# An attention GRU: its SBUF pools reordered, keys transposed two steps ahead, groups gathered a step ahead

## The chip, the cores and the metric

One core of a Trainium2 chip. The metric is the device time of one execution in microseconds (us), median of several runs. The experiments ran in three sessions, each on a chip of the same kind (called the second, third and fourth chip here; the record does not say whether one of them is the chip of the first measurement). Each session ran the kernel before beside the experiments, so only ratios within one chip are compared. All profiled runs quoted here were in the fast state (granted TensorE clock 0.994 to 0.996 over the whole execution).

## The reference, cut to what matters

For 1024 users with up to T = 100 past items each, a GRU runs over the items; its states are the *keys*. An attention gives each step a weight, and a second GRU, the AUGRU, runs over the keys:

```python
def augru_step(h, inp):
    x_t, a_t = inp                       # key and attention weight of step t
    ti = jnp.concatenate([h, x_t], axis=-1)
    r = jax.nn.sigmoid(ti @ aug_Wr.T + aug_br)
    u = jax.nn.sigmoid(ti @ aug_Wu.T + aug_bu)
    h_hat = jnp.tanh(jnp.concatenate([h * r, x_t], axis=-1) @ aug_Wh.T + aug_bh)
    u = a_t[:, None] * u
    h_new = (1.0 - u) * h + u * h_hat
    return (h_new, h_new)
```

The state after a user's last step goes, with other features, through three small layers to a score. Everything is in float32.

## The kernel before

The users are sorted by length and split into two halves of 512 (`NH = 2`), which take turns: a *half-step* is one step of one half. Ended users drop out on the right, so that a step works on `widths[t]` columns, from 512 down to 96. In the profiles a matmul in float32 stands as two records on the matmul engine (PE), each with a weight load (the page counts 8320 of each). Twelve of them make a half-step: `ph` is closed with `r` of the other half, then `pr` and `pu` with `h`, then three gates of the next half-step are opened with its key `k`.

```python
    def augru_phase(pools, widths, alive):
        wp = pools.enter_context(tc.tile_pool(name="wp3", bufs=3))
        qp = pools.enter_context(tc.tile_pool(name="qp3", bufs=3 * NH))
        sp = pools.enter_context(tc.tile_pool(name="sp3", bufs=2))
        kp = pools.enter_context(tc.tile_pool(name="kp3", bufs=4))

        ps = [
            pools.enter_context(tc.tile_pool(name=f"ps3_{n}", bufs=1, space=PSUM))
            for n in range(7)
        ]
        pa = pools.enter_context(tc.tile_pool(name="pa3", bufs=1, space=PSUM))
        # ... cut ...
        def load_key(t, i, n=None):          # cut: the first four lines
            k = qp.tile([P, HB], F32, name="k3")
            if q < WHOLE:                # steps 0 to 7: PE transposes, ACT copies
                p = pa.tile([P, HB], F32, tag="a", name="pk3") if n is None else bank("pk3", n)
                for g in range(-(-w // P)):
                    nc.tensor.transpose(p[:, ts(g, P)], r[:, g, ts(m, P)], ident)
                nc.scalar.copy(k[:, :w], p[:, :w])
            else:                        # from step 8 on: DVE transposes
                w = -(-w // R)
                nc.vector.transpose(
                    k.rearrange("p (k r) -> p k r", r=R)[:, :w, :], r[:, :w, ts(m, R)]
                )
            keys[t, i] = k
        # ... cut ...
        def half_step(t, i):
            w, h = widths[t], h3[i][:, : widths[t]]
            before, after = ((t - 1, 1), (t, 1)) if i == 0 else ((t, 0), (t + 1, 0))
            if before in resets:
                open_state(*before)
            pr = close_gate(t, i, "pr", wr, h)
            pu = close_gate(t, i, "pu", wu, h)
            nc.scalar.activation(pr, pr, AF.Sigmoid, bias=later["br"])
            nc.scalar.activation(pu, pu, AF.Sigmoid, bias=later["bu"])
            state = states.pop(1 - i, None)
            if state is not None:
                nc.vector.tensor_mul(state[0], state[0], state[1])
            r = wp.tile([P, HB], F32, name="r3")[:, :w]
            nc.vector.tensor_mul(r, h, pr)
            if state is not None:
                nc.vector.tensor_sub(state[3], state[0], state[2])
            if t == 1 and i == 0:
                store_weights(0, pa.tile([P, HB], F32, tag="a", name="pw"))
                first_state(1, spare)
            elif t == 1:
                first_weights(1, spare)
            nc.vector.tensor_mul(pu, pu, att.pop((t, i))[:, :w])
            rest = wp.tile([P, HB], F32, name="rest")[:, :w]
            nc.vector.scalar_tensor_tensor(
                out=rest, in0=pu, scalar=1.0, in1=h, op0=ALU.subtract, op1=ALU.mult
            )
            later["pace"] = rest[:, 0:1]
            resets[t, i] = r, pu, rest
            if after[0] < T and (*after, "pr") not in opened:
                open_gates(*after)
            if t == 1 and i:
                store_weights(1, spare)
            if t + 2 < T:
                load_att(t + 2, i)
            if 1 < t < T - 1:
                load_key(t + 1, i)
```

The tiles that the keys are transposed from (`rows`) come by indirect transfers that POOL issues (`gathers`), 32 for a group of eight steps, spread over the half-steps before. The GRU that runs before the AUGRU has its own pools; a tile of a new pool that lies over an old pool's space waits until that space is free (in the profile before, ACT's first key copy stands idle 8.44 us for POOL's `pooled`). Its six PSUM banks belong to one pool:

```python
        ps = pools.enter_context(tc.tile_pool(name="ps", bufs=6, space=PSUM))
```

Of the kernel before, what the change touches and what calls it, by code (L numbers as in the profile page):

```python
# [9 lines left out]
F32 = mybir.dt.float32  # L10
# [9 lines left out]
P = 128  # L20
B = 1024
T = 100
HB = 512
NH = B // HB
# [31 lines left out]
FIRST = [sum(READ[:q]) for q in range(len(READ))]  # L56
# [18 lines left out]
def kernel(ctx: ExitStack, tc: tile.TileContext, a: dict, out: bass.AP):  # L75
# [96 lines left out]
    def all_of(steps):  # L172
        for _ in steps:
            pass
# [762 lines left out]
    def augru_phase(pools, widths, alive):  # L937


        wp = pools.enter_context(tc.tile_pool(name="wp3", bufs=3))  # L940
        qp = pools.enter_context(tc.tile_pool(name="qp3", bufs=3 * NH))
        sp = pools.enter_context(tc.tile_pool(name="sp3", bufs=2))
        kp = pools.enter_context(tc.tile_pool(name="kp3", bufs=4))

# [11 lines left out]
        def bank(name, n=None):  # L956

            if n is None:
                n = ring.pop(0)
                ring.append(n)  # L960
            return ps[n].tile([P, HB], F32, tag="g", name=name)

        def first_step(i):

            k = keys.pop((0, i))
            gates = []
            for j, (n, f) in enumerate((("u", AF.Sigmoid), ("h", AF.Tanh))):
                p = bank(f"p{n}", EARLY_BANKS[NH * i + j])
                nc.tensor.matmul(p, lhsT=later["w" + n][:, 1, :], rhs=k, start=True, stop=True)
                gate = sp.tile([P, HB], F32, name=f"first_{n}")  # L970
                nc.scalar.activation(gate, p, f, bias=later["b" + n])
                gates.append(gate)
            return gates
# [18 lines left out]
        def first_state(i, p):  # L992
            weight_row(0, i, p)
            u, h = gates[i]
            nc.vector.tensor_mul(p, p, u)
            nc.vector.tensor_mul(h3[i], p, h)

        def first_weights(i, p):
            weight_row(1, i, p)
            at = att[1, i] = wp.tile([P, HB], F32, name="at", bufs=6)  # L1000
            nc.scalar.copy(at, p)

        def store_weights(i, p):

            for g in range(GH):
                nc.tensor.transpose(p[:, ts(g, P)], sorted_rows[i][:, g, :], ident)
            rows_t = wp.tile([P, HB], F32, name="att_t", bufs=2)
            nc.vector.tensor_copy(rows_t, p)
            nc.sync.dma_start(out=att_d[i], in_=rows_t[:T, :])
            load_att(2, i)  # L1010

        def load_att(t, i):
            w = widths[t]
            at = wp.tile([P, HB], F32, name="at", bufs=6)
            nc.sync.dma_start(
                out=at[:, :w], in_=att_d[i][t, :w].partition_broadcast(P)
            )
            att[t, i] = at

        def load_key(t, i, n=None):  # L1020

            q = max(j for j, first in enumerate(FIRST) if first <= t)
            w, m, r = widths[t], t - FIRST[q], rows[q, i]
            k = qp.tile([P, HB], F32, name="k3")
            if q < WHOLE:
# [4 lines that stand above are left out]
            else:  # L1030
# [6 lines that stand above are left out]
        def open_gates(t, i, banks=(None,) * 3):  # L1037

            k = keys.pop((t, i))[:, : widths[t]]
            for m, name, n in zip((wr, wh, wu), ("pr", "ph", "pu"), banks):  # L1040
                p = opened[t, i, name] = bank(name, n)[:, : widths[t]]
                nc.tensor.matmul(p, lhsT=m[:, 1, :], rhs=k, start=True, stop=False)

        def close_gate(t, i, name, m, v):
            p = opened.pop((t, i, name))
            nc.tensor.matmul(p, lhsT=m[:, 0, :], rhs=v, start=False, stop=True)  # L1046
            return p

        def open_state(t, i):

            r, u, rest = resets.pop((t, i))
            ph = close_gate(t, i, "ph", wh, r)
            c = wp.tile([P, HB], F32, name="c3")[:, : widths[t]]
            nc.scalar.activation(c, ph, AF.Tanh, bias=later["bh"])  # L1054
            states[i] = u, c, rest, h3[i][:, : widths[t]]
# [35 lines that stand above are left out]
                store_weights(1, spare)  # L1091
            if t + 2 < T:
                load_att(t + 2, i)
            if 1 < t < T - 1:
                load_key(t + 1, i)

        def last_state(i):
            u, c, rest, h = states.pop(i)
# [77 lines left out]
        def gathers(q):  # L1176
            for i in range(NH):
                yield from load_rows(q, i, widths[FIRST[q]], kp)

        def spread(q):  # L1180


            ahead = 2 if widths[FIRST[q]] > HB // 2 else 3
            n = NH * -(-widths[FIRST[q]] // R)
            slots = NH * (FIRST[q] - (FIRST[q - 1] if q > 2 else 1) - ahead)
            done = [-(-j * n // slots) for j in range(slots + 1)]
            return [b - a for a, b in zip(done, done[1:])]

# [14 lines left out]
        first_state(0, pa.tile([P, HB], F32, tag="a", name="first"))  # L1203
        first_weights(0, spare)
        ahead, due = gathers(2), spread(2)
        jobs, final = [], None
        for t in range(1, T):
            if t in FIRST[2:-1]:
                all_of(ahead)
                ahead, due = gathers(FIRST.index(t) + 1), spread(FIRST.index(t) + 1)  # L1210
            for i in range(NH):
                half_step(t, i)
                for _ in range(due.pop(0) if due else 0):
                    next(ahead, None)

                for n, job in enumerate(list(jobs)):
                    job[0] += 1
                    if n == 0 and job[0] > 2 * G and next(job[1], job) is job:
                        jobs.remove(job)
            left = alive[t + 1] if t + 1 < T else 0  # L1220
            for g in range(1, HB // PR):
                if left <= g * PR < alive[t]:
                    jobs.append([0, predict(g)])
                    if left:
                        next(jobs[-1][1])
            if t == T - G:
                final = predict(0, last=True)
                next(final)
# [10 lines left out]
    def augru(n):  # L1239
        with ExitStack() as pools, tc.manual_schedule():  # L1240
            augru_phase(pools, WIDTHS[n], ALIVE[n])
# [75 lines left out]
```

## Time and profile before

| | kernel before |
|---|---|
| time, median (range) | 2075.59 us (2075.27 to 2078.31, 3 runs) |
| profiled span | 2073.7 us |
| AUGRU starts (first key transposes on PE) | 1438.18 us |
| first gate, first weight gather, first `pr<-h`, after that | 11.51, 21.47, 29.87 us |
| half-steps 0 to 16, 16 to 120, 120 to 197 | 85.8, 369.1, 137.2 us |
| from the last half-step's start to the end | 13.5 us |

I number half-steps from 0 by the start of their `pr<-h`; half-step 120 is the first with about 216 columns, and 164 to 197 have 96. The rows add up to the span (1438.2 + 29.9 + 85.8 + 369.1 + 137.2 + 13.5 = 2073.7), so each later difference can be put into one of them. The lines that the argument starts from are shown in the prediction.

### The profile page before, as it was taken

To read this page: it belongs to the slowest core of one execution; us is meant where nothing else is said; L and a number is where in the kernel's file an instruction comes from. 1 tells how busy PE (TensorE), PEld (TensorE's weight loads), DVE (VectorE), ACT (ScalarE), POOL (GpSimd) and SP (SyncE) were. 2 spreads that over 40 slices of the span, in tenths; PEclk is the share of its full clock that TensorE was granted. 3 is DMA by queue.
4 is the path that set the end of the run, shared out by engine and by line. 5 is a ranking of instruction groups with operands and counts; after the bars stand their busy time and mean duration, and the time that the engine had idled before them with its cause. 6 is when DMAs were issued, how large, how long until landed. Compare 5 with 4: busy or idle time off the path is not lost. (4 is left out here: it accounts for less than half of the span.)

```text
span 2073.7 us, 26805 instructions
## 1 busy us (share of the span) xinstructions
PE 2037.9 (98%) x8320; PEld 980.9 (47%) x8320; DVE 1757.8 (85%) x3050; ACT 831.7 (40%) x1516; POOL 1306.9 (63%) x1306
## 2 busy tenths in 40 slices
PE   8999999999999999999999999997999999999998
PEld 3343333333333333333333333333444556679897
DVE  6888999998989898989889899999467777888886
ACT  3334343333334343334334334333444444445554
POOL 0234939669796959595978777998545444444332
PEclk9999999999999999999999999999999999999999
DMA  4632333322334333333332233342434333333321
GB/s 116 118 93 89 102 103 96 101 80 91 107 111 103 109 113 115 102 111 109 115 98 86 84 103 96 94 121 89 118 94 116 92 93 97 98 97 102 84 73 35
DMA packets 254324, 205.09 MB, mean 99 GB/s; under 512 B 75814, under 2 KB 216842, under 8 KB 254170
## 3 DMA queue, kind: packets, MB, share of 16 engines
q1 hardware_dynamic: 240266, 170.64, 28.8%
q0 software_dynamic: 12320, 32.44, 5.5%
q8 instruction: 68, 1.11, 0.2%
q14 instruction: 86, 0.70, 0.1%
q10 hardware_dynamic: 1584, 0.20, 0.1%
HBM read 147.16 MB, written 54.40 MB: 97 GB/s over the span
## 5 line engine op out<-in xcount | busy, mean ns | idle before, releaser
L495 PE MATMUL ps<-x,wih 128*128 128x512 f32 x1200 | 592.3, 603 | 3.9 <-DMA x<-in_hist_x 3.9
L495 PE MATMUL ps<-hn,whh 128*128 128x512 f32 x1188 | 574.4, 592 | 0.0
L495 PEld LDWEIGHTS ps<-x,wih 128*128 128x128 f32 x1200 | 220.7, 190 | 327.2 <-issue 251.4
L495 PEld LDWEIGHTS ps<-hn,whh 128*128 128x128 f32 x1188 | 225.7, 190 | 284.2 <-issue 275.1
L481 POOL TENSOR_TENSOR xm<-x,m 128x512 f32<-128x512 f32 x200 | 247.4, 1237 | 137.9 <-DMA m<-mask_d 137.6
L526 ACT ACTIVATE ps<-ps,bih 128x512 f32<-128x512 f32 x200 | 132.4, 662 | 491.2 <-DVE ps L525 491.2
L507 ACT ACTIVATE r<-ps,brz 128x512 f32<-128x512 f32 x200 | 137.5, 688 | 370.0 <-PE ps L495 369.3
L482 POOL TENSOR_TENSOR hist<-hist,xm 128x512 f32<-128x512 f32 x200 | 266.9, 1334 | 15.7
L594 POOL TENSOR_TENSOR pooled<-pooled,kw 128x512 f32<-128x512 f32 x191 | 254.6, 1333 | 15.0
L593 POOL TENSOR_TENSOR kw<-kt,e 128x512 f32<-128x512 f32 x191 | 219.4, 1149 | 64.7 <-DVE e L766 64.6
L164 POOL DMA_INDIRECT rows<-keys_d,idx_k x208 | 202.8, 975 | 83.6 <-POOL rows L163 51.4
L570 DVE TENSOR_TENSOR kq<-hn,item 128x512 f32<-128x512 f32 x200 | 230.3, 1191 | 0.0
L657 PE MATMUL pm<-hn,wk 128*32 128x512 f32 x1200 | 212.8, 598 | 3.5 <-ACT q L238 2.0
L657 PE MATMUL pm<-kq,wkq 128*32 128x512 f32 x1200 | 210.4, 594 | 0.0
L1054 ACT ACTIVATE c<-ph,bh 128x96 f32<-128x96 f32 (+42 forms) x198 | 96.9, 489 | 262.9 <-PE ph L1046 232.0
L657 PE MATMUL pm<-mv,w 128*32 128x512 f32 (+1 forms) x808 | 196.5, 598 | 1.5 <-DVE e L747 1.5
L163 POOL COPY rows<-rest 128x1 f32<-128x1 f32 x208 | 39.5, 190 | 214.6 <-DVE rest L1083 209.7
L1070 DVE TENSOR_TENSOR pu<-pu,c 128x96 f32<-128x96 f32 (+42 forms) x197 | 88.9, 451 | 99.7 <-ACT c L1054 90.4
L691 DVE TENSOR_TENSOR f<-pm,q 128x512 f32<-128x512 f32 x200 | 128.4, 684 | 51.1 <-PE pm L657 50.9
L530 DVE TENSOR_TENSOR d<-hn,ps 128x512 f32<-128x512 f32 x198 | 136.1, 687 | 34.8 <-ACT ps L526 32.4
L525 DVE TENSOR_TENSOR ps<-ps,u 128x512 f32<-128x512 f32 x200 | 140.0, 700 | 21.5 <-PE ps L495 0.5
L531 DVE TENSOR_TENSOR d<-ps,d 128x512 f32<-128x512 f32 x200 | 138.4, 692 | 23.4 <-ACT ps L527 6.2
(180 smaller groups left out, 3029.3 us busy)
## 6 DMA issues: line engine op xcount, KB each, us to landing
x<-in_hist_x SPq DMA_DIRECT2D x212, 256.0 KB
keys_d<-kt SPq DMA_DIRECT2D x46, 1024.0 KB
m<-mask_d SPq DMA_DIRECT2D x200, 128.0 KB
keys_d<-kt SPq DMA_DIRECT2D x64, 64.0 KB
rows<-keys_d,idx_k POOLq DMA_INDIRECT x208
s_b<-mv SPq DMA_DIRECT2D x200, 8.0 KB
mask_i<-in_mask SPq DMA_DIRECT2D x8, 200.0 KB
at<-att_d SPq DMA_DIRECT2D x32, 48.0 KB
```

What stands on the lines that cost most here:

```text
L164: nc.gpsimd.indirect_dma_start(out=r[:, k, :], out_offset=None, in_=keys_d[q], in_offset=bass.IndirectOffsetOnAxis(ap=idx_k[:, k, i : i + ...
L481: nc.gpsimd.tensor_mul(d, x, m)
L482: nc.gpsimd.tensor_add(acc, acc, d)
L495: nc.tensor.matmul(p, lhsT=w[:, g, :], rhs=v, start=(j == 0), stop=(j == len(parts) - 1),)
L507: nc.scalar.activation(r, pr, AF.Sigmoid, bias=brz[:, 0:1])
L525: nc.vector.tensor_add(pi, pi, u)
L530: nc.vector.tensor_sub(d, h, pi)
L531: nc.vector.tensor_mul(d, pz, d)
L570: nc.vector.tensor_mul(kq, h, item[:, self.cols])
L593: eng.tensor_mul(d, k, w)
L594: eng.tensor_add(acc, acc, d)
L657: nc.tensor.matmul(p[i][s, :], lhsT=w[:, s], rhs=v, start=start, stop=stop)
```

## The change

Its intent: the keys and first gates of the AUGRU shall not wait for the end of the GRU's pooling (part a), no key shall be made only just before the matmuls that read it (part b), and the groups are gathered a step earlier to serve that (part c). The diff, blank lines left out:

```diff
     def augru_phase(pools, widths, alive):
+        qp = pools.enter_context(tc.tile_pool(name="qp3", bufs=3 * NH))
+        fp = pools.enter_context(tc.tile_pool(name="fp3", bufs=NH))
         wp = pools.enter_context(tc.tile_pool(name="wp3", bufs=3))
-        qp = pools.enter_context(tc.tile_pool(name="qp3", bufs=3 * NH))
         sp = pools.enter_context(tc.tile_pool(name="sp3", bufs=2))
@@ first_step
-                gate = sp.tile([P, HB], F32, name=f"first_{n}")
+                gate = fp.tile([P, HB], F32, name=f"first_{n}")
@@ half_step
-            if 1 < t < T - 1:
-                load_key(t + 1, i)
+            if t + 2 < T:
+                load_key(t + 2, i)
@@ spread
-            ahead = 2 if widths[FIRST[q]] > HB // 2 else 3
+            ahead = 3 if widths[FIRST[q]] > HB // 2 else 4
             n = NH * -(-widths[FIRST[q]] // R)
-            slots = NH * (FIRST[q] - (FIRST[q - 1] if q > 2 else 1) - ahead)
+            slots = NH * (FIRST[q] - (FIRST[q - 1] - 1 if q > 2 else 1) - ahead)
@@ the loop over t
-            if t in FIRST[2:-1]:
+            if t + 1 in FIRST[2:-1]:
                 all_of(ahead)
-                ahead, due = gathers(FIRST.index(t) + 1), spread(FIRST.index(t) + 1)
+                ahead, due = gathers(FIRST.index(t + 1) + 1), spread(FIRST.index(t + 1) + 1)
```

## The prediction

> **What bounds the kernel now.** I read the page first, then each engine's timeline across the change from GRU to AUGRU, then the waits and the timeline of the narrow AUGRU steps. The page's first part:
>
> ```profile
> PE 2037.9 (98%) x8320; PEld 980.9 (47%) x8320; DVE 1757.8 (85%) x3050; ACT 831.7 (40%) x1516; POOL 1306.9 (63%) x1306
> ```
>
> The matmul engine has work nearly all the time, so what counts is where it stands still or its starts slip. The change touches only the AUGRU, from about 1438 us on. Two places matter. The first is the seam, from the timelines of PE, ACT, DVE and POOL:
>
> ```profile
> 1438.18 1.04 PE L1028 MATMUL pk<-ident,rows 128*128 128x128 f32 x8
> 1449.68 2.07 PE L969 MATMUL pu<-k,wu 128*128 128x512 f32 x2 [10.47 <-ACT k L1029]
> ...
> 1464.50 0.93 PE L984 MATMUL first<-ident,att_r 128*128 128x128 f32 x6 [0.68 <-issue]
> 1465.98 0.49 PE L984 MATMUL first<-ident,att_r 128*128 128x128 f32 x2 [0.55 <-DMA att_r<-pooled_d,idx]
> ```
> ```profile
> 1449.05 1.07 ACT L1029 COPY k<-pk 128x512 f32<-128x512 f32 x2 [8.44 <-POOL pooled L594]
> ```
> ```profile
> 1448.50 0.69 DVE L594 TENSOR_TENSOR pooled<-pooled,last 128x512 f32<-128x512 f32 x1
> ```
> ```profile
> 1459.65 0.99 POOL L140 DMA_INDIRECT att_r<-pooled_d,idx  x1 [10.63 <-DMA pooled_d<-s_b]
> ```
>
> The first keys are transposed on PE by 1439.2, but ACT may copy them to SBUF only at 1449.05, when POOL's last L594 is done: their buffers lie over the GRU's work tiles. PE then stands idle 10.5 us. What ends the seam, though, is another chain: the pooled sums are stored, POOL gathers them from 1459.65, and PE's L984 waits for that gather at 1465.98.
>
> The second place is the narrow steps. From the waits of the weight loads between 1868 and 2063, and the timeline around 1985 (134 of 512 columns alive):
>
> ```profile
> PEld pr L1042 <- DVE k L1032: 4.5, 16, 0.4
> ```
> ```profile
> 1984.56 0.42 PE L1046 MATMUL ph<-r,wh 128*128 128x138 f32 x2
> ...
> 1985.02 0.38 ACT L1054 ACTIVATE c<-ph,bh 128x138 f32<-128x138 f32 x1 [0.66 <-PE ph L1046]
> 1985.05 0.39 PE L1046 MATMUL pu<-h,wu 128*128 128x134 f32 x2
> 1985.10 0.33 DVE L1032 STREAM_TRANSPOSE k<-rows 128x160 f32<-128x160 f32 x1
> ...
> 1985.29 0.34 ACT L1066 ACTIVATE pr<-pr,br 128x134 f32<-128x134 f32 x1
> ...
> 1985.49 0.50 PE L1042 MATMUL pr<-k,wr 128*128 128x134 f32 x2
> ...
> 1985.66 0.30 DVE L1072 TENSOR_TENSOR r<-h,pr 128x134 f32<-128x134 f32 x1
> ```
>
> DVE transposes a key at the very end of a half-step, and PE's next matmul but none reads it: pr<-k starts 0.06 us after the transpose ends at 1985.43, instead of 0.23 us after pu<-h started. Only waits over 0.15 us are listed, so 4.5 us is too small a figure. I counted it otherwise: from every matmul record's start to the next one's, less that record's undisturbed cadence (columns over 1190 per us, as the 384-wide pairs go at 0.645 us a pair, and never under 0.112 us, as the 96-wide ones go). Between 1476 and 1868 us nothing is left over: PE alone sets the pace. Between 1868 and 2053 us 15.0 us are left: 11.7 at pr<-k (6.8 before its first record, 4.9 before its second, whose weights were not loaded ahead either), 3.1 at ph<-r, 1.0 at pu<-k. Of the 6.8, all but a few hundredths of what I could match stands within 0.1 us of a transpose's end.
>
> [...] the undisturbed 128-wide loads cost nothing beside the 0.23 us per matmul, but where the matmul waits, the pair pr<-k takes 0.50 us against 0.39. [...] granted clock 0.50 for 1449.0 to 1451.5 and 0.58 to 1453.0, and the first gate's pair takes 2.07 us.
>
> **The change, part by part.** No instruction is added or removed; both built programs have the same counts on each engine.
>
> (a) Pools. Keys and first gates now lie over the GRU's inputs, whose last reader is PE's L624, done at 1438.3. ACT's first key copy loses its wait for POOL and can run behind ACT's own last GRU work (1440.6), some 8.4 us earlier; the 1.28 us table load hides too. But the built changed program still has PE's first gate wait for DVE's last L594: its PSUM bank belongs to a GRU pool that is released as a whole. That ends at 1449.19. So PE can start at about 1449.25, not 1449.68: 0.43 us, and still cold. The stores of the pooled sums that ACT issues behind the first gates, then the gathers and L984, move by the same 0.4 us. Worth 0.4 us.
>
> (b) Keys two steps ahead. Key 3 is transposed at t=1 rather than 2, where PE otherwise stands 0.67 us before a pr<-h (that wait is on the new state). One group of four PE transposes (four at 0.11 us) goes into that hole: 0.4 us. The later PE transposes only move. From key 8 on DVE transposes them, and in the changed program pr<-k has no wait for DVE left at all: the key was made three half-steps before. So the 11.7 us at pr<-k go. What comes back depends on the next limit, the recurrence from ph to the next ph. At 134 columns: ph to tanh start 0.46 (1984.56 to 1985.02), to the sigmoid 0.27, to r 0.37, r itself 0.30, on to PE 0.06: 1.46 us. PE's own floor is 12 records of 0.115 = 1.37 us, and the half-steps there last 1.80, 1.54, 1.69, 1.55, mean 1.65. At 96 columns the bare recurrence shows at the end, where no gates are opened any more: 1.32 us (2059.96 to 2061.28), against PE's 12 x 0.112 = 1.35 and a usual pair of 1.49 and 1.39. [...] So I let return 0.08 us in each of the 20 half-steps between 150 and 108 columns (1.6 us), 0.02 in the 37 narrower ones (0.7), and 0.7 around the early predictions. That is 3.0 back, 8.7 net.
>
> (c) Gathers a step ahead. They keep their distance to the transposes: both move one step. Only the first group is squeezed, 32 gathers into 8 half-steps rather than 10. POOL needs about 1.44 us each, 5.8 us for four against half-steps of 5.5. It falls some 2 us behind by the eighth (1521), and the first transpose of that group stands near 1528. Worth 0.
>
> Sum: 0.4 + 0.4 + 8.7 = 9.5 us of 2075.6, so **2066 us**, 0.5% faster.
>
> **Rivals.** *The wait moves on to ph<-r.* For it: 1.46 against 1.37 at 134 columns, DVE's six operations need about 1.43 there too, and early predictions disturb the order. Then half of the 11.7 returns: some 2071. Against it: at 96 columns recurrence and PE are even[...]. *The seam opens fully.* If the bank wait did not bind, the gates would start 8 us sooner, and ACT would issue its stores when the sums are ready (1450.5); with SP's five issued by 1452.4, the gathers would start near 1454.8: 4.9 us instead of 0.4, about 2061.5. Against it stands that wait in the changed program. *The squeezed gathers stall key 8.* If POOL fell back further, PE would wait about 5 us, once: 2071. Against it: 7 us of slack.
>
> **Range and chances.** Between rival two and rival one lie 2061 and 2071; repeat runs spread 3 us. I take that as the range. For 2% the change would have to move 41 us; the whole stretch from the seam to the end shows only some 17 us of slipped starts and about 10 idle us. Faster 0.01, same 0.98, slower 0.01.
>
> **What would show each step.** (a) ACT's first L1029 copy near 1441, yet PE's first gate at 1449.2 to 1449.3, and POOL's first weight gather near 1459.2. If that gather starts before 1456, I am wrong there. (b) No wait of pr<-k for DVE; the leftover at pr<-k from 11.7 to under 1; that at ph<-r from 3.1 to about 6; half-steps at 96 columns near 1.36. If ph<-r takes over 8, rival one holds. (c) No wait of DVE's first key transpose for a gather. Half-steps over 210 columns must keep their length to 0.02 us; if they don't, something I haven't seen is at work.

## The result, and the profile after

| | before | after |
|---|---|---|
| time, median (range, runs) | 2075.13 us (2074.15 to 2078.31, 6) | 2069.05 us (2066.83 to 2069.98, 6) |
| profiled span | 2073.7 | 2067.4 |
| AUGRU starts | 1438.18 | 1436.42 |
| first gate, weight gather, `pr<-h` after that | 11.51, 21.47, 29.87 | 11.11, 22.12, 30.50 |
| half-steps 0 to 16 | 85.8 | 86.7 |
| half-steps 16 to 120 | 369.1 | 369.1 |
| half-steps 120 to 197 | 137.2 | 131.3 |
| end | 13.5 | 13.4 |

The ratio of the times is 0.9968 (95% interval 0.9955 to 0.9981). A ratio here is the one on record, over the fast runs; it is not quite the ratio of the medians in the table. The change gained 6 us, 0.3%: less than the 2% that would count as faster, less than the 9.5 us predicted, inside the range.

Of the 6.3 us between the two spans, 1.8 lie in the GRU, which the change does not touch (the eleven other profiles start the AUGRU between 1435.7 and 1439.7 us, whatever the kernel). The narrow half-steps from 120 on gave 5.9; the seam and the first half-steps took 1.5 back.

The seam after, from the timelines of ACT, DVE and PE (columns: start, duration, engine, line, operation, tiles, shapes; in brackets the idle time before and what ended it):

```profile
1439.33 1.07 ACT L1031 COPY k<-pk 128x512 f32<-128x512 f32 x2 [0.48 <-ACT part L632]
1440.42 1.28 ACT L973 ACT_TABLE_LOAD   x1
```
```profile
1446.74 0.69 DVE L594 TENSOR_TENSOR pooled<-pooled,last 128x512 f32<-128x512 f32 x1
```
```profile
1436.42 1.04 PE L1030 MATMUL pk<-ident,rows 128*128 128x128 f32 x8
1447.53 2.04 PE L971 MATMUL pu<-k,wu 128*128 128x512 f32 x2 [10.08 <-issue]
```

ACT's copies no longer wait for POOL: they stand 2.9 us after the transposes began, not 10.9. Yet PE's first gate starts at 1447.53, 0.10 us after DVE's last L594 ended (1446.74 + 0.69): PE was idle 10.1 us all the same, and the view names no releaser ("issue"). That it waits for the end of a pool is what the experiment with separate banks below tests.

The narrow half-steps after, at 96 columns, from the timelines of PE, ACT and DVE of a second profile of the changed kernel (on a chip without the stalls that are told of below; the 96-column median is the same in the first):

```profile
2009.88 0.43 PE L1048 MATMUL ph<-r,wh 128*128 128x96 f32 x2
2010.15 0.39 PE L1048 MATMUL pr<-h,wr 128*128 128x96 f32 x2
2010.38 0.39 PE L1048 MATMUL pu<-h,wu 128*128 128x96 f32 x2
2010.60 0.39 PE L1044 MATMUL pr<-k,wr 128*128 128x96 f32 x2
2010.83 0.39 PE L1044 MATMUL ph<-k,wh 128*128 128x96 f32 x2
2011.05 0.39 PE L1044 MATMUL pu<-k,wu 128*128 128x96 f32 x2
2011.27 0.43 PE L1048 MATMUL ph<-r,wh 128*128 128x96 f32 x2
```
```profile
2010.36 0.34 ACT L1056 ACTIVATE c<-ph,bh 128x96 f32<-128x96 f32 x1 [0.56 <-PE ph L1048]
2010.60 0.31 ACT L1068 ACTIVATE pr<-pr,br 128x96 f32<-128x96 f32 x1
```
```profile
2010.35 0.27 DVE L1034 STREAM_TRANSPOSE k<-rows 128x96 f32<-128x96 f32 x1
2010.73 0.27 DVE L1072 TENSOR_TENSOR pu<-pu,c 128x96 f32<-128x96 f32 x1
2010.93 0.26 DVE L1074 TENSOR_TENSOR r<-h,pr 128x96 f32<-128x96 f32 x1
```

`pr<-k` at 2010.60 follows `pu<-h` by 0.22 us, its plain cadence: it waits for no transpose. The pair that is longer now is `ph<-r`, 0.43 us against 0.39: it starts 0.08 us after `r` ends (2011.19). From one `ph<-r` to the next the chain is 0.48 to the tanh, 0.24 to the sigmoid of `pr`, 0.33 to `r`, 0.26 for `r` and 0.08 to PE, 1.39 us in sum, against twelve PE records of 0.112, 1.345.

I counted the leftover of PE as in the prediction (start to start less the undisturbed cadence), now over half-steps 120 to 197 of every profile, so that the same piece of the program is compared:

| us of leftover | all | `pr<-k` | `ph<-r` | `pu<-k` |
|---|---|---|---|---|
| before | 15.6 | 12.2 | 3.0 | 1.0 |
| after | 9.7 | 0.0 | 7.2 | 3.2 |

The lines do not add up to "all" exactly, since the small matmuls of the early predictions run a little below the cadence I assumed. The whole `pr<-k` term went, as predicted; 6.4 us came back in the other two columns, where I had expected 3.0.

### The profile page after: what moved, and what is told of

Its sections match the earlier page's. It is cut to its first block, busy times and chain, and to the rows that moved or that the text cites. A ratio compares the mean times of both kernels' runs of the same rounds, so it can differ in the third digit from the quotient of the medians.

```text
span 2067.4 us, 26811 instructions
## 1 busy us (share of the span) xinstructions
PE 2029.8 (98%) x8320; PEld 978.9 (47%) x8320; DVE 1755.2 (85%) x3050; ACT 831.5 (40%) x1516; POOL 1304.8 (63%) x1306
## 5 line engine op out<-in xcount | busy, mean ns | idle before, releaser
L507 ACT ACTIVATE r<-ps,brz 128x512 f32<-128x512 f32 x200 | 137.4, 687 | 371.1 <-PE ps L495 370.2
L594 POOL TENSOR_TENSOR pooled<-pooled,kw 128x512 f32<-128x512 f32 x191 | 254.3, 1332 | 15.0
```

Of the source, the lines that this page charges most:

```text
L507: nc.scalar.activation(r, pr, AF.Sigmoid, bias=brz[:, 0:1])
L594: eng.tensor_add(acc, acc, d)
```

## The experiments

Theory: (a) is worth next to nothing because a whole PSUM pool of the GRU must be free before the first gate; (b) makes the gain by taking `pr<-k`'s wait away, and gives part of it back to the recurrence through `r`; (c) costs nothing. Rivals: DVE's queue as a whole, not the chain, is what comes back; the squeezed gathers of (c) cost the time that is missing.

### Part (a) alone

```diff
-            if t + 2 < T:
-                load_key(t + 2, i)
+            if 1 < t < T - 1:
+                load_key(t + 1, i)      # and spread and the loop as before
```

> The kernel before with only the new pool order. Theory (the seam is held by the PSUM wait and by the stores, so the pools buy next to nothing): within 1 us of the kernel before, half-steps unchanged, PE's first gate 11.1 us after the GRU's last key transposes start instead of 11.5 us, ACT's first key copy about 9 us earlier. Rival (the pools bring a good part of the 6 us): 2 us or more faster than before.

On this second chip the kernel before took 2082.17 us (2080.72 to 2087.46, 11 runs); this and the next three kernels ran beside it.

Measured: 2083.47 us, ratio 1.0003 (0.9991 to 1.0015). The first gate came 11.11 us after the first transposes as in the changed kernel, the half-steps at 96 columns kept the median of before (1.490 against 1.489 us), and the leftover at `pr<-k` stayed (12.8 us). "Half-steps unchanged" failed otherwise: 16 to 120 took 371.1 us and 120 to 197 took 142.8, with stalls of the kind told of below under "The changed kernel again"; there is no profile of the kernel before on this chip to compare with. So the pools' order by itself gains nothing that can be measured, and has no part in the narrow steps.

### Parts (b) and (c) alone

```diff
-        qp = pools.enter_context(tc.tile_pool(name="qp3", bufs=3 * NH))
-        fp = pools.enter_context(tc.tile_pool(name="fp3", bufs=NH))
         wp = pools.enter_context(tc.tile_pool(name="wp3", bufs=3))
+        qp = pools.enter_context(tc.tile_pool(name="qp3", bufs=3 * NH))      # cut: the first gates back in sp
```

> The changed kernel with the old pool order: keys two steps and gathers one step ahead, alone. Theory: the gain is the wait of pr<-k in the narrow steps, so 5 to 6.5 us faster than before, with 210-to-108 half-steps summing to 74.6 us and the narrower ones to 56.7 us as in the changed kernel. Rival (pools bring a third): 4 us faster at most.

Measured: 2074.69 us, ratio 0.9960 (0.9947 to 0.9973), which is no less than the whole change gave on the first chip (the whole change did not run on this one). The gain, 7.5 us between the medians, is above the 5 to 6.5 expected, while the two stretches of half-steps took 76.2 and 57.8 us, not 74.6 and 56.7. The half-steps at 96 columns had the median of the changed kernel, 1.388 us, `pr<-k` had no leftover (0.0), and the first gate started 11.50 us after the transposes, as before. The profiled run had one flaw in the first sixteen half-steps: the ninth lasted 7.33 us instead of 5.45.

### Key 3 transposed where it was before

Keys of step 3 at t = 2, together with those of step 4; everything else as changed. It tests whether key 3 at t = 1 fills a hole, and whether it caused the longer first half-step of the changed kernel (6.28 us against 4.97).

```diff
+            if t == 2:
+                load_key(3, i)
-            if t + 2 < T:
+            if 1 < t < T - 2:
                 load_key(t + 2, i)
```

> The changed kernel, but key 3 is transposed at t=2 together with key 4, no longer at t=1. Theory (key 3's PE transposes at t=1 wait for DVE's copy of the attention weights, because both use the one bank of the same pool, and hold ph<-r behind them): the first 16 half-steps shrink from 86.7 to 85.8 us or less, 0.9 us faster than the changed kernel, some 7 us faster than before. Rival (transposes are only moved, the longer start is chance): first 16 half-steps stay at 86.7 us and the time stays.

Measured: 2076.71 us, ratio 0.9965 (0.9951 to 0.9979). What I had expected of the first half-step failed: it lasted 6.42 us without key 3 in it, as it did in the kernel with part (a) alone (6.42). Other profiles settle that this is a matter of the run: the changed kernel again, on another chip, took 4.96 us, the kernel before 4.97 and 5.21. The next three half-steps took 8.28, 6.92 and 6.95 us, against 7.00, 5.59 and 5.57 in the changed kernel. In the second and third of them two groups of transposes share one PSUM bank within a half-step, and the second group waits for ACT's copy of the first; that is 2.7 us. The first of them is another matter: its `pr<-h` and `pu<-h` pairs took 1.88 and 1.91 us in place of 1.02, at a granted clock of 0.55 from 1473.6 to 1477 us. So this is no clean removal of one effect: of the 4.1 us that its first sixteen half-steps are longer, 2.7 are of its own making and 1.3 go with the clock.

The hole itself shows in the half-steps of before and of the changed kernel. In both profiles of each kernel, half-step 1 went from 6.59 to 7.00 and 7.02, and half-steps 10 and 11 from 5.39 and 5.37 to 4.95 and 4.93. Of the two key groups of about 0.44 us that left half-steps 10 and 11, one is paid for in half-step 1. If the other is free, 0.45 us are gained, as predicted (0.4). It would have to show in half-step 0, and that varies too much from run to run to tell: 4.96 to 6.71 us in the nine profiles with key 3 there (mean 5.8), 4.97 to 6.42 in the four without (mean 5.8). The means agree, so a free group fits, to no better than some tenths.

### The GRU's PSUM banks released one by one

If the first gate waits for a pool that is released as a whole, six pools of one bank each must let it start. The banks that the first gates use are chosen so that those read last by the GRU come last.

```diff
-EARLY_BANKS, LATE_BANKS = (2, 5, 6, 0), (3, 4, 1)
+EARLY_BANKS, LATE_BANKS = (3, 5, 6, 0), (2, 4, 1)
-        ps = pools.enter_context(tc.tile_pool(name="ps", bufs=6, space=PSUM))
+        ps = Banks()       # six pools of one bank, whose tile() takes them in turn
```

> The changed kernel, with the GRU's six PSUM banks as six pools of one, so that a bank is free for the AUGRU when its own last reader is done. Theory (the first gate waits for DVE's last pooled sum only because the banks are released together): PE's first gate some 4 us after the last key transposes start, instead of 11.1; ACT is through with the first gates before the sums are ready, its stores go out at once, POOL's first weight gather starts 17 to 18 us after those transposes instead of 22.1; 3.5 to 5 us faster than the changed kernel. Rival (the stores and gathers take their time whatever the gates do): under 1 us.

Measured: 2069.83 us, ratio 0.9935 (0.9923 to 0.9947). The first gate started 3.55 us after the transposes instead of 11.11, the first weight gather 17.37 instead of 22.12, the first `pr<-h` 26.19 instead of 30.50, so 4.3 us at the seam as expected. Against the kernel before on this chip it gains 12 us; the changed kernel did not run here, so that "3.5 to 5 us faster" than it can only be checked on the third chip, below. But its ninth half-step took 9.06 us and its tenth 5.84 (a later expectation counts from 0 and calls them eighth and ninth), some 4 us over the usual 5.45 and 5.42, and with the flaw in the run of (b) and (c) alone this made the squeezed gathers suspect.

### The changed kernel again

> The changed kernel again, unaltered, beside the other runs of this chip. If the 0.9968 of the first measurement holds, the ratio to the kernel before lies between 0.995 and 0.998. Its profile should again show the half-steps at 96 columns at a median of 1.387 us, no wait of pr<-k for DVE, the first gate 11.1 us and the first weight gather 22 us after the first key transposes, and the sixteen first half-steps at 86 to 88 us unless a gather stalls them.

Measured, on a third chip: 2062.67 us (2061.47 to 2063.37) against 2070.76 (2068.38 to 2071.56), ratio 0.9959 (0.9946 to 0.9973). The ratio, the first gate (11.11 us) and the missing wait of `pr<-k` are as expected; the first weight gather came after 21.35 us and the first sixteen half-steps took 85.4, both a little less than expected. But half-steps 120 to 197 took 125.4 us against 131.3 in the first profile. All of that difference lies in a few half-steps: 130 to 132, 144 and 145, 164, 167 and 168, 180 and 181, and 193; the 96-column median is the same (1.388 and 1.387). There ACT starts a tanh or a sigmoid late. Half-step 145, ACT's and PE's timelines of the first profile:

```profile
1972.39 0.36 ACT L1069 ACTIVATE pu<-pu,bu 128x148 f32<-128x148 f32 x1 [0.43 <-PE pu L1044]
1974.56 0.38 ACT L1056 ACTIVATE c<-ph,bh 128x148 f32<-128x148 f32 x1 [1.81 <-PE ph L1044]
```
```profile
1972.36 0.52 PE L1048 MATMUL ph<-r,wh 128*128 128x148 f32 x2
...
1973.46 0.41 PE L1044 MATMUL ph<-k,wh 128*128 128x144 f32 x2
1975.00 0.51 PE L1044 MATMUL pu<-k,wu 128*128 128x144 f32 x2 [1.12 <-ACT c L1056]
```

and ACT's of the second profile, where the same tanh starts 1.03 us after the sigmoid before it started, not 2.17:

```profile
1969.42 0.36 ACT L1069 ACTIVATE pu<-pu,bu 128x148 f32<-128x148 f32 x1
1970.45 0.38 ACT L1056 ACTIVATE c<-ph,bh 128x148 f32<-128x148 f32 x1 [0.67 <-PE ph L1048]
```

The tanh reads `ph`, whose last record ends at about 1972.9; the view puts the wait down to a later matmul. The views do not print when PE reports its finished matmuls, but the packed trace has it: the semaphore on which ACT waits for PE was updated at 1971.58, 1972.31, 1973.05, 1973.78, 1973.83 and 1974.54, then four times more, 0.04 us apart. In the second profile the updates come 0.25 to 0.33 us apart. The tanh starts 0.02 us after the update at 1974.54, and all late tanhs in all profiles start 0.02 or 0.03 us after an update, just as those that are on time do. So what is late is PE's report and not ACT. Whether the matmul itself ended late or only its report came late is not shown, since the ends of matmuls are modelled in the profile. PE's `pu<-k` then waits 1.12 us for the bank that the tanh frees.

All four profiles of the third chip (the quiet chip below) are free of such late reports, and the nine others have them, the kernel before too (half-steps 121, 132 to 134, 153, 180 and 181 in its profile). A tanh usually starts 0.31 us after the start of the last `ph` record, or after the end of the ACT instruction before it if that is later. What late ones take beyond that sums to 4.6 us before and 4.3 us after between half-steps 120 and 197. What the late reports cost PE differs, and comes below.

### No late keys, and `ph` without `r`

Two kernels that are wrong on purpose tell the recurrence from a full DVE queue. (Both were still within the tolerance of the comparison with the reference, which says that the comparison is blind to such errors in the last, narrow steps, not that they are right.)

```diff
+            if q >= WHOLE and w <= 216:
+                keys[t, i] = later["old_key", i]
+                return      # cut: the last transposed key is kept as "old_key"
```

> Wrong on purpose: from 216 columns down no key is transposed any more, an old one is read. DVE loses one of its six operations per half-step, PE keeps all of its matmuls. Theory one (what came back at ph<-r is the recurrence ph, tanh, sigmoid, r, ph, through ACT's and DVE's queues, in which the transpose has no part since it lies after r and is done before the next r can start): the half-steps at 96 columns stay at a median of 1.385 to 1.390, the leftover at ph<-r between 1868 and 2053 us stays at 7 to 9.5 us. Theory two (DVE's queue is full, the transpose delays u*c and r): the median falls to 1.345 to 1.36, ph<-r to under 3 us, and the time by 4 us or so.

```diff
-            ph = close_gate(t, i, "ph", wh, r)
+            ph = close_gate(t, i, "ph", wh, r if widths[t] > 216 else h3[i][:, : widths[t]])
```

> Wrong on purpose: from 216 columns down ph is closed with h in place of r; r is still computed, so ACT and DVE do the same work, but PE's ph no longer waits for r. Theory one (the recurrence through r): half-steps at 96 columns fall from 1.387 to PE's floor, 12 x 0.112 = 1.345 (1.345 to 1.355), the leftover at ph<-r goes from 7 to 9.5 us to under 1, and its second record takes the usual 0.112 again; the time falls by 5 to 9 us against the changed kernel. Theory two (ACT or DVE as a whole are the bound, not the chain): a wait of the same size appears at pr<-h or pu<-k instead and the half-steps stay at 1.38 or more.

All of these ran on the chip of the second profile of the changed kernel; the leftovers and lengths are of half-steps 120 to 197:

| | time | length | `ph` | `pr<-h` | median, 96 columns |
|---|---|---|---|---|---|
| changed kernel | 2062.67 us | 125.4 | 4.4 | 0.0 | 1.388 |
| no late keys | 2062.28 | 125.3 | 4.0 | 0.3 | 1.385 |
| `ph` from `h` | 2059.94 | 123.0 | 0.3 | 1.8 | 1.340 |

Without its transposes (0.27 us each at 96 columns, one of DVE's six operations of a half-step) nothing changes, 1.385 us against 1.388: its queue is not the bound. Without the wait for `r`, the half-steps at 96 columns fall to PE's floor at once:

```profile
2008.82 0.39 PE L1048 MATMUL ph<-h,wh 128*128 128x96 f32 x2
...
2010.16 0.39 PE L1048 MATMUL ph<-h,wh 128*128 128x96 f32 x2
```

1.34 us from one to the next, and the pair takes 0.39 us again. So theory one holds: what came back at `ph<-r` is the chain through ACT and DVE. Of my numbers, the leftover at `ph<-r` (7 to 9.5 us) and the time (5 to 9 us less) missed: on this chip there were only 4.4 us at `ph<-r` to take away, and 1.8 us reappeared at `pr<-h`, chiefly between 150 and 108 columns, where the next chain, through the new state, stands close behind. The gain was 2.7 us; the ranges of the two times overlap (2061.47 to 2063.37 and 2058.33 to 2063.12), so the half-steps carry this reading and not the time.

### The gathers over ten half-steps, with the banks apart

```diff
-            ahead = 3 if widths[FIRST[q]] > HB // 2 else 4
+            ahead = 2 if q == 2 else 3 if widths[FIRST[q]] > HB // 2 else 4
```

> The kernel e4_banks_apart with its first group of gathers spread over ten half-steps again, as in the kernel before, not eight. Theory (squeezing four gathers into a half-step stalls the eighth and ninth half-steps, 9.06 and 5.84 us in e4 against 5.2 elsewhere): the half-steps 0 to 16 fall from 89.7 to about 86, no half-step after the fourth lasts over 5.7 us, and the ratio to the kernel before falls from 0.9935 to 0.9915 to 0.9925. Rival (that stall is chance, or DMA traffic that comes anyway): ratio 0.993 to 0.9945, and a stall of 2 us or more may show anywhere in the first 16, or nowhere. At the seam nothing changes: first gate 3.6 us, first weight gather 17.4 us after the first key transposes.

Measured on the same chip: 2058.49 us (2057.78 to 2059.46), ratio 0.9942 (0.9928 to 0.9955), 4.2 us under the changed kernel there, as expected of separate banks. The first sixteen half-steps took 86.4 us, and none from the third on was over 5.6, but the ratio is not in the range of the theory; it is in that of the rival. To decide, both versions and the kernel before ran once more on one chip, a fourth.

> The kernel before as a control: ratio 1 within 0.15%. On this chip too, the leftover at pr<-k between 1868 and 2053 us should be near 11.7 us and the half-steps at 96 columns near 1.49 us, the first gate 11.5 us and the first weight gather 21.5 us after the first key transposes; the first half-step may last from 5.0 to 6.4 us without the change having a part in it, since the changed kernel alone showed 4.96 and 6.28.

> The kernel e4_banks_apart once more, unaltered, beside the version with ten half-steps of gathers, on one chip. If squeezing the first gathers into eight half-steps stalls the ninth half-step, its profile shows a half-step of over 6 us there again and its ratio to the kernel before stands 0.001 or more above that of the other. If the stall in the first run was chance, the half-steps 2 to 16 last 5.6 to 4.8 us without a break and the two ratios agree within 0.001.

> The version with the GRU's PSUM banks apart and ten half-steps of gathers once more: ratio to the kernel before 0.993 to 0.9945, no half-step from the third to the sixteenth over 5.7 us.

| | median | ratio (interval) | half-steps 120 to 197 |
|---|---|---|---|
| kernel before | 2075.28 us | 1.0003 (0.9988 to 1.0019) | 136.9 |
| banks apart, eight half-steps | 2064.24 | 0.9946 (0.9933 to 0.9960) | 131.0 |
| banks apart, ten half-steps | 2064.60 | 0.9947 (0.9934 to 0.9961) | 131.5 |

The two agree to 0.0001, and the ninth half-step of the version with eight lasted 5.45 us this time. So the squeezed gathers cost nothing here. The traces of the two stalls say what it was: in the ninth half-step of the banks-apart version on the second chip a key's transposes ended at 1507.71, ACT copied them only at 1512.76, 0.02 us after a late report of PE, and PE waited 2.07 us for the tanh behind that copy; in the kernel with parts (b) and (c) alone the copy stood 3.6 us after its transposes. No gather was waited for. The control again had its leftover of 12.3 us at `pr<-k` and its 1.487 us at 96 columns; its first weight gather came after 22.59 us, not 21.5. On this chip the late reports were back, at half-steps 131, 145, 167, 180 and 181 in both versions, whose half-steps from 120 on took 5.7 and 6.1 us longer than those of the changed kernel on the third chip.

The seam with banks apart, PE's timeline from the third chip:

```profile
1437.33 1.04 PE L1042 MATMUL pk<-ident,rows 128*128 128x128 f32 x8
1440.86 1.12 PE L983 MATMUL pu<-k,wu 128*128 128x512 f32 x2 [2.50 <-ACT k L1043]
...
1461.09 0.80 PE L998 MATMUL first<-ident,att_r 128*128 128x128 f32 x2 [0.24 <-DMA att_r<-pooled_d,idx]
1461.68 1.91 PE L998 MATMUL spare<-ident,att_r 128*128 128x128 f32 x8
1463.48 2.07 PE L1060 MATMUL pr<-h,wr 128*128 128x512 f32 x2
```

and POOL's, whose gathers follow each other every 1.26 us, as in the kernel before, but start earlier:

```profile
1454.70 0.99 POOL L140 DMA_INDIRECT att_r<-pooled_d,idx  x1 [6.54 <-ACT k L1043]
```

The gates hide beside the pooling, 7.6 us earlier than in the changed kernel on that chip. The first weight gather comes only 4.0 us earlier and the first `pr<-h` 3.6. Until the gathered weights come PE is busy for 2.89 of the 7 us from 1455 to 1462, at a granted clock of 0.79; from 1462 to 1475 the granted clock is 0.85, and the first `pr<-h` takes 2.07 us. In the changed kernel on that chip PE is busy for 6.13 of the first 7 us, the granted clock is 1.00 in both stretches, and `pr<-h` takes 1.12. At half-step 16, which starts 112.5 us after the transposes, and 115.2 in the changed kernel, 2.7 us are left.

## Why the prediction was right or wrong

- **Part (a), 0.4 us: right.** The first gate moved from 11.51 to 11.11 us after the transposes, in every profile with the new pools; the copy of ACT moved 8 us without effect. Of the 0.4 nothing can be seen in the time (ratio 1.0003 for (a) alone), and the gather that follows varies more from run to run (21.35 and 22.12 after, 21.47 and 22.59 before). The named cause, the PSUM pool released as a whole, is shown by the version that releases its banks one by one. Rival two was rightly excluded for this change, and its size, 4.9 us, was about that of this version (4.1 to 5.3 at the gather, against the two profiles of before).
- **Key 3 in a hole, 0.4 us: fits.** It is 0.45 us if half-step 0 has not grown, and that half-step varies by more than this from run to run.
- **The wait of `pr<-k`, 11.7 us: right.** It is 12.2 in the longer piece counted here, and it went wholly.
- **What comes back, 3.0 us: the term that was mis-sized.** It was 6.4 us in the first profile (4.2 at `ph<-r`, 2.2 at `pu<-k`). Two things are in it. First, the recurrence is a little longer than I let it be: I gave it 0.02 us a half-step at 96 columns, from its bare length near the end (1.32), where no gates are opened; in the full half-step it is 1.388 against a floor of 1.345, so 0.04 (I had said half-steps near 1.36), and between 150 and 108 columns the quiet profile has 2.5 us where I had 1.6. That wider half-steps would give nothing back was my estimate. On the quiet chip `ph<-r` has 4.4 us in all. Of the 3.0 that it had before, 2.1 stand in half-steps with late reports of PE, so that the recurrence had 0.9, and some 3.5 us came back through it. This is an estimate, as there is no profile of the kernel before without late reports. Second, the late reports: at these two places they cost 5.9 us after (10.4 against 4.5 on the quiet chip) and about 3.0 before (2.1 and 0.9), so 2.9 more. I had not looked for them and left no room. Their places differ between the kernels: half-step 145, the longest, is late in all six profiles with part (b) off the quiet chip and in none of the three without. So the change may have a part in where they fall.
- **By chip.** Ratio 0.9959, about 8.5 us, on the chip without late reports; 0.9968, 6.6 us, on the first. The intervals overlap, and there is no profile of the kernel before on the quiet chip, so that the late reports account for the difference between prediction and result is likely, and not shown. The medians point the same way: the kernel before is 4.4 us faster there than in the first measurement, the changed one 6.4, which would make 2 us more of late reports after; but that compares two sessions. Why reports are late, and why not on one chip, stays open.
- **Part (c), nothing: right.** DVE's first transposes waited for no gather, and eight or ten half-steps made no difference on the fourth chip.
- **Rival one** (the wait moves on to `ph<-r`) was right in kind: that is where the leftover went, 7.2 us of 9.7. My own mark for it, over 8 us, is reached in three profiles of experiments with part (b) (8.9 to 10.0) and not in the others (7.6 and 7.7 with late reports, 4.4 without). Its time was summed wrongly: with half of the 11.7 us (5.9) back and 0.8 from the other parts it comes to 2068.9 us, not to "some 2071". The measured 2069.05 lies on that sum by luck, since 2.9 of the 6.4 us that came back are late reports and no recurrence.
- **The check on wide half-steps** held: half-steps 16 to 120 took 369.1 us in both kernels.

## What to carry to other kernels

When a wait is removed from an engine's queue, work out the next chain from end to end, with the durations in the full loop and not from a stretch where the loop is emptier: here it stood 3% above the engine's floor. A tile moved to earlier free SBUF space gained nothing here (ratio 1.0003) while the same step waited for a PSUM pool that is released as a whole; look for the last such wait before moving buffers. And compare half-steps by number between profiles of several chips, of the kernel before too: a few that are late on one chip and not on another decide how much of a gain is seen, and before a chain of the program is blamed for them, look at when the engine that is waited for reported.

## What else the traces show

- A late operand cost PE more here than the wait itself. At 96 columns the pair `ph<-r` takes 0.43 instead of 0.39 us, and 3.6 of the 4.4 us at `ph<-r` in the quiet profile stand before the second record of the pair, and are gone (0.3 left in all) when `ph` does not wait.
- In the version with banks apart and ten half-steps, as first profiled, PE was busy for 0.95 of the 3.86 us from 1455.24 to 1459.10, never idle for more than 2.25 us at a stretch, and from 1459.1 to 1462 the granted clock was 0.50; the next full matmul pair took 2.07 us instead of 1.12.
- At half-step 145 of the first profile of the changed kernel, PE's reports come as five semaphore updates within 0.16 us, after gaps of about 0.73: the tanh there starts 1.1 us later than on the quiet chip, and half-steps 120 to 197 take 5.9 us more, with the same program. The trace has instruction transfers of 0.3 to 1.4 us in both profiles, at the same places, and none that starts between 1958.3 and 1978.6 us, around the stall at 1974. So these are not shown to be the cause.
